# Image 0's mirrored runs moved to other steps, column sums in two chains of transfers, closings of layer 2 added from PSUM

## The chip, the cores and the metric

The kernel runs on one core of one Trainium2 chip. The metric is the device time of one execution in microseconds (us), the median of several runs. The engines are named as in the profile: PE (matmul), PEld (the loading of weights into PE), DVE (vector), ACT (activation), POOL (GpSimd) and SP (here a queue of DMA issues).

## The reference

Four images of 64 x 64 positions with 64 channels, float32, go through four layers one after the other:

```python
# layer 0: attention over the 4096 positions of an image, with q, k, v projections
energy = einsum('bic,bjc->bij', q, k); x = gamma * softmax(energy) @ v + x
# layer 1: a block of norm, pointwise, 3x3 depthwise taps, gate, channel scale, pointwise, and
#          a second half of norm, pointwise, gate, pointwise, each added to x
# layer 2: attention of the image with itself: softmax(x @ x.T) @ x, added to x
# layer 3: a non-local block (theta, phi, g projections), then a batch norm over all images
```

In layer 2 the scores are the product of x with itself, so the block of queries g against keys h is the transpose of the block of queries h against keys g. The kernel uses this: the exponential of one block serves both.

## The kernel before, in words

**Order of the work.** The kernel is a list of items that a schedule (lines 1790 to 1830) writes out by hand. Items 0 to 127 are layer 0, 32 per image. Layer 1 of an image is a generator that runs in a lane called `conv` inside the items that follow; each `yield` states how many us of item time are to pass before its next part. Layer 1 of image 3, the last one, runs inside image 0's layer 2. A second lane, `misc`, holds `features2` (keys of layer 2, tile `ko`), which are started at the item given in `misc_from`. Then come layer 2 of image 0, and layers 2 and 3 of the images by turns: 2(1), 3(0), 2(2), 3(1), 2(3), 3(2), 3(3).

**Layer 2.** The positions are cut into 8 parts. `PART` (image 0) and `FULL` (images 1 to 3) list, for each part h, which other parts are taken against it. A plain number g is one block that counts once; a pair in brackets is a mirrored run, whose blocks count for h and, transposed, for the two parts of the pair. Each number gives two steps, each pair four; image 0 has 100 steps and seven runs, the others 72 steps and fourteen runs each. `item(n)` (1484) issues for step n:

- `score(n)`: 4 matmuls (L1384; 8 records in the profile) into a PSUM slot of 128 x 1024, and two exponentials on ACT (L1389, with row sums) into half of an `e` tile. The slots are taken by turns (`new_ps`), and a matmul into a slot waits for the last reader of what was there.
- for a step of a run, `turned(n)`: a DVE transpose (L1402) into a `turned` tile; and `column_sums(n)`: in image 0 a DMA from POOL's queue that adds the exponentials into `esum` (L1417), in the others a POOL addition (L1419); after the last step of h one POOL addition joins the halves (L1421).
- `products(n)`, two steps later (three for the first of an h): 4 matmuls (L1440) into accumulators. At the end of an h the accumulators are copied or added to `A` (ACT copies at L1448 and, for image 0, L1451; DVE additions at L1454).
- `turned_products(run)`: 64 matmuls (L1465; 128 records) from the `turned` tile into two PSUM slots, and four DVE evacuations into `A` (L1478 additions, L1480 copies for the first visit). Within the pass the first two matmuls write the first slot and the next two the second one. Their other operand is `xr`, which `weights(h)` fetches in 16 transfers on SP (L1361) at the steps in `weights_at`.
- `spread_sums(h)`: a DVE transpose and a reduction of `esum` (L1429, L1430).

```python
for run, (_, _, last) in enumerate(runs):
    if n - (3 if b and run == 0 else 2) == last:
        turned_products(run)
```

**Pools.** `e`, `esum`, `own`, `xr` and layer 0's exponentials share a ring of six tiles, taken by turns. `turned`, `A`, `ko` and others share a ring of five big tiles. In image 0 the first six runs use one `turned` tile and the last another; in the other images two alternate. `t` tiles come from a ring of two.

**Layer 1 inside image 0's layer 2.** The depthwise taps are DVE instructions (L1240, with L1243 and L1251 as the last of a row), for r = 1 and then r = 0; `ytot` (L1257) sums their results, and a matmul at L1260 reads it. The second half is a norm (matmuls at L1170, transfers into `xn` at L1183) and pointwise matmuls (L1205), a DVE gate into `u` (L1288) and a matmul at L1292.

**Closing.** `close2(b)` (1517) finishes an image's layer 2 four blocks of 128 x 1024 at a time: 8 PE transposes of `A` into a PSUM slot (L1542), a DVE multiply by the reciprocal sums into a `t` tile (L1543), and two DVE additions to X (L1549). Images 0 to 2 are closed at items 12, 22, 32 and 42 of the next image's layer 2, two steps ahead of a turned pass; image 3 inside layer 3 of image 2.

Of the kernel before, what the change touches and what calls it, by code (L numbers as in the profile page):

```python
# [10 lines left out]
ALU = mybir.AluOpType  # L11
# [680 lines left out]
def fast_path(ctx: ExitStack, tc: tile.TileContext, a: dict, out: bass.AP, bad):  # L692
    nc = tc.nc
# [298 lines left out]
    def at(i, fn):  # L992
        due.setdefault(i, []).append(fn)
# [165 lines left out]
    def norm(x, y):  # L1159


        sq = [new_t("sq"), new_t("sq")]
        for i in range(2):
            act(sq[i], x[:, bass.ts(i, 1024)], AF.Square)
        yield 4.5
        ps = new_ps()
        for i, src in enumerate(((x, x), (sq[0], sq[1]))):
            for j in range(4):
                c = 512 * j if i == 0 else 512 * (j % 2)
                mm(  # L1170
                    ps[32 * j : 32 * j + 32, bass.ts(i, 512)], jsel, src[j // 2][:, c : c + 512],
                    start=True, stop=True,
                )
        t = new_t()
        act(t[:, 0:512], ps[:, 0:512], AF.Square)
        stt(t[:, 0:512], t[:, 0:512], -1.0, ps[:, 512:1024], ALU.mult, ALU.add)
        yield 4.0
        act(t[:, 0:512], t[:, 0:512], AF.Ln, bias=eps1)
        act(t[:, 512:1024], t[:, 0:512], AF.Exp, scale=-0.5)
        yield 3.0  # L1180
        for j in range(4):
            for h in range(2):
                nc.sync.dma_start(  # L1183
                    out=y[64 * h : 64 * h + 64, bass.ts(j, 512)],
                    in_=t[32 * j + 16 * h : 32 * j + 16 * h + 16, 512:1024]
                    .unsqueeze(1).to_broadcast([16, 4, 512]),
                )
        yield 11.0
        for jp in range(2):
            cols = bass.ts(jp, 1024)  # L1190
            nc.vector.tensor_mul(y[:, cols], y[:, cols], x[:, cols])
            yield 1.8
# [6 lines left out]
    def layer1(b):  # L1199
# [76 lines left out]
            nc.vector.tensor_add(xs, xs, t[:, 0:512])  # L1276
            yield 3.0
        z = xn.tile([128, 2048], F32, tag="xn", name="xn")
        yield from norm(x, z)
        for j in range(4):  # L1280
            t, u = new_t(), new_t("u")
            for r in range(2):
                ps = new_ps()
                pointwise(ps, pw3, r, z, j)
                if r == 0:
                    act(t, ps, AF.Identity, bias=pwb[:, 1, 0:1])
                else:
                    stt(u, ps, pwb[:, 1, 1:2], t, ALU.add, ALU.mult)  # L1288
                yield 6.0 if r else 4.0
            ps = new_ps()  # L1290
            for s in range(2):
                mm(ps[64 * s : 64 * s + 64, 0:512], pw4, u[:, bass.ts(s, 512)], start=True, stop=True)  # L1292
            act(t[:, 0:512], ps[:, 0:512], AF.Identity, bias=resb[:, 1:2], scale=V("L1_conv_gamma"))
            xs = x[:, bass.ts(j, 512)]
            nc.vector.tensor_add(xs, xs, t[:, 0:512])
            yield 3.0
# [3 lines left out]
    def features2(b):  # L1300
# [13 lines left out]
    SIDES = [[(7, (h + 1) % 7), ((h + 2) % 7, (h + 3) % 7)] for h in range(7)]  # L1314
    FULL = [(7, [7])] + [(h, [h] + SIDES[h]) for h in range(6)] + [(6, SIDES[6] + [6])]
    PART = [
        (0, [0, 5, (1, 2), 6, 7, (3, 4)]), (1, [1, 2, 3, 4, 7]), (2, [2, 1, 3, 4, 7]), (3, [3, 1, 2, 4]),
        (4, [4, 1, 2, 3]), (7, [7, 0, 5, 6, 1, 2, (3, 4)]), (6, [6, 0, (1, 2), 5, 7, (3, 4)]),
        (5, [5, 0, (1, 2), 6, (3, 4), 7]),
    ]  # L1320

    def layer2(b, when_free=None):
# [16 lines left out]
        m.first = [4 * sum(m.count[:g]) for g in range(8)]  # L1339
        m.mirrored = [h for h, _ in (PART if b == 0 else FULL) if mine_t[h]]  # L1340
        begin = [mine[h][0] for h in range(8)]
        spread_at = {mine_t[h][-1] + 5: h for h in m.mirrored}
        late_start = 4 if b else 6
        used, todo, seen = {}, [], set()
        st = {"e": {}, "T": {}, "esum": {}}

        def tile_of(run):
            return run % 2 if b else run // (len(runs) - 1)

        def slot(g, t):  # L1350
            k = used[g, t] = used.get((g, t), -1) + 1
# [12 lines left out]
                    )  # L1364

        if b == 0:
            weights_at = {0: 0, 24: 7, 44: 6, 74: 5}
        else:
            weights_at = {6: 0, 8: 1, **{mine[h][0] - 1: h for h in range(2, 7)}}

# [35 lines left out]
        def column_sums(n):  # L1406
            h, _, _, run, _ = steps[n]
            if run is None:
                return
            k, e = mine_t[h].index(n), st["e"][n]  # L1410
            if k == (0 if b == 0 else 1):
                st["esum"][h] = new_e("esum")
            if h not in st["esum"]:
                return
            esum = st["esum"][h][:, 0:1024]
            if b == 0:
                nc.gpsimd.dma_start(out=esum, in_=e, **({} if k == 0 else {"accum_op": ALU.add}))  # L1417
            else:
                nc.gpsimd.tensor_add(esum, st["e"][mine_t[h][0]] if k == 1 else esum, e)  # L1419
            if n == mine_t[h][-1]:  # L1420
                nc.gpsimd.tensor_add(esum[:, 0:512], esum[:, 0:512], esum[:, 512:1024])  # L1421
# [61 lines left out]
        def item(n):  # L1483
            if n in weights_at:
                weights(weights_at[n])
            score(n)
            turned(n)
            column_sums(n)
            todo.append(n)
            if n == 2:  # L1490
                m.A = new_big("A")
            if b == 0:
                follow(0)
                conv.tick(3.1)
                misc.tick(1.8)
            if n >= late_start:
                for _ in range(2):
                    if todo and todo[0] <= n - (3 if b == 0 and todo[0] in begin else 2):
                        products(todo.pop(0))
            for run, (_, _, last) in enumerate(runs):  # L1500
                if n - (3 if b and run == 0 else 2) == last:
                    turned_products(run)
                    if run == len(runs) - 2 and when_free:
                        when_free()
            if n == len(steps) - 1:
                while todo:
                    products(todo.pop(0))
            if n in spread_at:
                spread_sums(spread_at[n])
# [2 lines left out]
            items.append((lambda n=n: item(n), 1.6 if b else 0.0))  # L1512
        for n, h in spread_at.items():
            if n >= len(steps):
                at(len(items) + (1 if b else 6), lambda h=h: spread_sums(h))

    def close2(b):
        x, m = X[:, b], im[b]
        ps, tot, n = piece(), sums2[:, b, :], 4 * max(m.mirrored) + 4
        cs = m.cs.rearrange("p (j k) -> p j k", k=4)  # L1520
        for k in range(4):
            mm(ps[32 * k : 32 * k + 32, 0:n], sel4, cs[:, 0:n, k], start=True, stop=True)
        g = 0
        while g < 8:
            k = g
            while k < 8 and m.count[k] == m.count[g]:
                k += 1
            nc.vector.tensor_reduce(
                tot[:, 4 * g : 4 * k],
                m.zs[:, m.first[g] : m.first[g] + 4 * m.count[g] * (k - g)]  # L1530
                .rearrange("p (t k) -> p t k", k=m.count[g]), AX.X, ALU.add,
            )
            g = k
        nc.vector.tensor_add(tot[:, 0:n], ps[:, 0:n], tot[:, 0:n])  # L1534
        rz = sm.tile([128, 32], F32, tag="rz2", name="rz2")
        nc.vector.reciprocal(rz, tot)
        yield
        for i in range(4):
            ps, t = new_ps(), new_t()
            for j in range(8):  # L1540
                c = 1024 * i + 128 * j
                nc.tensor.transpose(ps[:, bass.ts(j, 128)], m.A[:, c : c + 128], ident)  # L1542
            nc.vector.tensor_mul(  # L1543
                t.rearrange("p (j n) -> p j n", n=128), ps.rearrange("p (j n) -> p j n", n=128),
                rz[:, bass.ts(i, 8)].unsqueeze(2).to_broadcast([128, 8, 128]),
            )
            xs = x[:, bass.ts(i, 512)].rearrange("p (j h) -> p j h", h=H)
            for o in range(2):
                nc.vector.tensor_add(xs, xs, t.rearrange("p (j o h) -> p j o h", j=8, o=2)[:, :, o, :])  # L1549
            yield  # L1550


# [251 lines left out]
    for b in range(B):  # L1804
        misc_to[len(items)] = True
        f = len(items)
        if b == 0:
            layer2(b)
            misc_from[f + 74] = [features2(b + 1)]
        else:  # L1810
            layer2(b, lambda b=b: keys3(b - 1))
            turns = close2(b - 1)
            for i in (8, 12, 22, 32, 42):
                at(f + i, lambda turns=turns: next(turns))
            misc_from[f + 46] = [open3(b - 1)]
            f = len(items)
            misc_to[f] = True
            layer3(b - 1)
            if b + 1 < B:
                turns = features2(b + 1)  # L1820
                for i in (4, 7, 10, 13):
                    between3[f + i] = 2, lambda turns=turns: next(turns)
# [221 lines left out]
```

## Time and profile before

| | |
|---|---|
| time, median of 3 runs | 2458.18 us (2457.44 to 2460.28) |
| profiled execution, its own time | 2460.18 us |
| span of the profiled execution | 2458.3 us |
| PE busy | 2414.6 us, 98% of the span |
| ACT, DVE, POOL busy | 67%, 60%, 21% |
| granted PE clock, mean | 0.996 |
| image 0's layer 2 | 1018 to 1277 us of the span |

The span runs from the first to the last instruction; the execution's own time has about 2 us around it. Busy time of PE is modelled, and matmuls overlap in it, so what a stall or an instruction costs is read from starts: a score or product of one step is 0.86 us of PE, a step that has nothing else 1.72 us. In a list of waits the columns are the waiting engine and line, what it waited for, the total, the number of times and the longest. In a timeline they are the start, the duration, the engine, line and operation, output and input, a count, and in brackets the idle time ahead of it with what ended it.

### The profile page before, as it was taken

Reading aid. Unit: us, or ns where it says so; the run is one execution under the profiler, and the core shown is the slowest. Engines: PE = TensorE matmul, PEld = TensorE weight load, DVE = VectorE, ACT = ScalarE, POOL = GpSimd, SP = SyncE. Lnnn points to the kernel's source line nnn. Section 1 sums busy time; section 2 is a strip of 40 time slices with the busy share of each in tenths; the row PEclk is TensorE's granted clock in tenths of the full one; section 3 lists DMA queues with packets and bytes.
Section 4 is the critical chain, followed back from the end, with each engine's and each line's share of the span. In section 5 each row is a group of like instructions: output and inputs, shape, how many; then the busy total and the mean of one; then the engine's idle time right before and its main releaser. Section 6 shows DMA issues by size and latency. Waiting matters only on the chain.

```text
span 2458.3 us, 63648 instructions
## 1 busy us (share of the span) xinstructions
PE 2414.6 (98%) x27509; PEld 932.0 (38%) x27509; DVE 1471.1 (60%) x1785; ACT 1648.8 (67%) x3144; POOL 528.0 (21%) x379
## 2 busy tenths in 40 slices
PE   9999999999999999999899999999999999999998
PEld 3343453336433633335334442144431244421113
DVE  2010377227822773278547757877668876678886
ACT  4666766676666666678454449964479844579996
POOL 2000000000000000000127662247631365622110
PEclk9999999999999999999999999999999999999999
DMA  3000000000000000230540017610065400296554
GB/s 79 1 18 1 19 1 18 18 19 1 18 18 18 2 19 18 50 65 18 112 102 22 19 45 155 135 31 19 20 138 118 91 19 20 68 174 139 121 117 117
DMA packets 67094, 134.31 MB, mean 55 GB/s; under 512 B 12941, under 2 KB 34166, under 8 KB 66806
## 3 DMA queue, kind: packets, MB, share of 16 engines
q0 software_dynamic: 23744, 84.46, 17.2%
q1 hardware_dynamic: 42309, 43.85, 7.9%
q8 instruction: 218, 3.57, 0.6%
q10 hardware_dynamic: 752, 1.85, 0.2%
q14 instruction: 71, 0.57, 0.1%
HBM read 4.80 MB, written 4.19 MB: 4 GB/s over the span
## 4 chain that ended last, share of the span: by engine, by line
PE 85%; DVE 7%; ACT 4%; DMA 2%; issue 1%; SPq 0%; POOL 0%; ACTq 0%; DVEq 0%; POOLq 0%
PE PS L1121 18%; PE PS L1095 18%; PE PS L1384 9%; PE PS L1440 9%; PE PS L1627 8%; PE PS L1688 8%; PE PS L1465 7%; PE PS L1205 2%; DVE tg L1679 2%; DVE y L1240 2%; ACT e L1638 2%; DMA xn<-e 1%; ACT e L1389 1%; DVE turned L1402 1%; ACT e L1100 1%
## 5 line engine op out<-in xcount | busy, mean ns | idle before, releaser
L1100 ACT ACTIVATE e<-PS 128x1024 f32<-128x1024 f32 x512 | 523.6, 1023 | 332.3 <-PE PS L1095 299.6
L1389 ACT ACTIVATE e<-PS 128x512 f32<-128x512 f32 x632 | 370.8, 595 | 350.8 <-PE PS L1384 330.6
L1121 PE MATMUL PS<-e,vq 64*64 64x512 f32 x4096 | 577.2, 592 | 0.0
L1095 PE MATMUL PS<-X,q 64*64 64x512 f32 x4096 | 574.9, 590 | 1.8 <-DVE X L979 1.7
L1638 ACT ACTIVATE e<-PS 128x512 f32<-128x512 f32 (+2 forms) x588 | 500.1, 921 | 58.3 <-PE PS L1627 35.8
L1679 DVE TENSOR_TENSOR tg<-tg,e 128x2048 f32<-128x2048 f32 x172 | 393.9, 2290 | 42.8 <-ACT e L1638 31.4
L1384 PE MATMUL PS<-ko 64*64 64x512 f32 x2528 | 343.4, 596 | 2.9 <-DVE A L1480 2.0
L1440 PE MATMUL PS<-e,X 64*64 64x512 f32 x2528 | 339.7, 594 | 1.4 <-DVE X L1133 0.6
L1240 DVE SCALAR_TENSOR_TENSOR y<-pad,vec,y 128x1024 f32<-128x1024 f32 x240 | 307.9, 1283 | 14.8 <-ACT y L1236 7.4
L1419 POOL TENSOR_TENSOR esum<-esum,e 128x1024 f32<-128x1024 f32 x126 | 298.9, 2372 | 49.3 <-ACT e L1389 42.3
L1402 DVE STREAM_TRANSPOSE turned<-e 128x1024 f32<-128x1024 f32 x196 | 241.0, 1238 | 114.0 <-ACT e L1389 114.0
L1627 PE MATMUL PS<-tg,ph 32*64 32x512 f32 x4096 | 294.9, 612 | 1.4 <-ACT e L1638 1.2
L1417 POOL DMA_DIRECT2D esum<-e x28 | 23.1, 827 | 1222.3 <-ACT e L1389 1171.4
L1095 PEld LDWEIGHTS PS<-X,q 64*64 64x64 f32 x4096 | 184.0, 133 | 258.9 <-issue 178.5
L1121 PEld LDWEIGHTS PS<-e,vq 64*64 64x64 f32 x4096 | 184.1, 133 | 252.0 <-issue 158.7
L1688 PE MATMUL PS<-e,tg 128*32 128x512 f32 x2048 | 272.5, 604 | 0.0
L1108 DVE TENSOR_REDUCE sums<-zs 128x1 f32<-128x4 f32 x128 | 19.6, 153 | 260.6 <-ACT e L1100 260.4
L1440 PEld LDWEIGHTS PS<-e,X 64*64 64x64 f32 x2528 | 105.6, 134 | 171.2 <-issue 148.3
L1660 POOL DMA_DIRECT2D xn<-e x116 | 101.1, 897 | 289.9 <-ACT e L1638 205.0
L1384 PEld LDWEIGHTS PS<-ko 64*64 64x64 f32 x2528 | 98.0, 133 | 164.3 <-issue 135.2
L1465 PE MATMUL PS<-turned,xn 32*64 32x256 f32 x5376 | 156.3, 377 | 0.5 <-DVE sums L1534 0.5
L1627 PEld LDWEIGHTS PS<-tg,ph 32*64 32x64 f32 x4096 | 63.4, 129 | 222.5 <-ACT e L1638 191.5
(217 smaller groups left out, 1685.0 us busy)
## 6 DMA issues: line engine op xcount, KB each, us to landing
xn<-e POOLq DMA_DIRECT2D x132, 512.0 KB, 5.2
esum<-e POOLq DMA_DIRECT2D x28, 512.0 KB, 4.6
xn<-X SPq DMA_DIRECT2D x336, 32.0 KB
xn<-t SPq DMA_DIRECT2D x64, 128.0 KB
ph<-tg SPq DMA_DIRECT2D x64, 128.0 KB
ko<-ko SPq DMA_DIRECT2D x32, 128.0 KB
xr<-in_x_dram SPq DMA_DIRECT2D x13, 256.0 KB
q<-q SPq DMA_DIRECT2D x12, 256.0 KB
```

Of the source, the lines that this page charges most:

```text
L1095: mm(ps[64 * c : 64 * c + 64, bass.ts(r, 512)], m.q[rows_, 128 * t + 64 * c : 128 * t + 64 * c + 64], x[rows_, bass.ts(g, 512)], start=Tru ...
L1100: act(es[g // 2][:, bass.ts(g % 2, 1024)], ps, AF.Exp, bias=SHIFT0, accum_out=zs[:, g : g + 1],)
L1121: ins = mm(PS[64 * s : 64 * s + 64, 2048 + 512 * j : 2560 + 512 * j], vq[rows_, :], es[j // 2][rows_, k : k + 512], start=t == 0 and i < 2 ...
L1240: stt(y1, win, wt, y1, ALU.mult, ALU.add)
L1384: mm(ps[64 * c : 64 * c + 64, bass.ts(r, 512)], m.ko[rows_, k : k + 64], m.ko[rows_, bass.ts(h, 512)], start=True, stop=True,)
L1389: act(e[:, bass.ts(r, 512)], ps[:, bass.ts(r, 512)], AF.Exp, bias=SHIFT2, accum_out=slot(g, 2 * u + r),)
L1440: mm(st["acc"][r][64 * c : 64 * c + 64, :], xw[rows_, 4 * g + 2 * u + c, :], st["e"][n][rows_, bass.ts(c, 512)], start=n == mine[h][0], st ...
L1465: mm(slots[q // 2][64 * c : 64 * c + 64, o : o + 256], st["xr"][rows_, w : w + 64], T[rows_, bass.ts(e, 256)], start=e < 2, stop=e >= 14,)
L1627: mm(PS[64 * c : 64 * c + 64, bass.ts(banks[k], 512)], m.ph[32 * k : 32 * k + 32, 128 * mc + 64 * c : 128 * mc + 64 * c + 64], m.th[32 * k ...
L1638: act(e[:, 512 * lo : 512 * k], PS[:, 512 * banks[lo] : 512 * banks[lo] + 512 * (k - lo)], AF.Exp,)
L1679: nc.vector.tensor_add(esum, esum, e)
L1688: mm(st["y"][32 * k : 32 * k + 32, :], m.gx[:, i % 32, :], es[i][:, bass.ts(k, 512)], start=mc == 0, stop=i % 32 == 31,)
```

## The change

Seven things change, all but the last in image 0's layer 2:

1. `PART` orders the blocks anew. The runs before end at steps 7, 15 (h 0), 67 (h 7), 75, 83 (h 6), 91 and 97 (h 5); afterwards at 5, 13 (h 0), 23 (h 1), 77, 83 (h 6), 91 and 97 (h 5). The number of blocks, steps and runs in the table is the same.
2. Two `turned` tiles alternate, and each turned pass is issued three steps after its run's last step instead of two. The last step of the layer is 99.
3. The weights are fetched at steps 0, 10, 40 and 50.
4. The column sums of an h go by turns to two halves of `esum`, two chains of transfers, and one more transfer joins them: 32 issues instead of 28. `spread_sums` comes nine steps after the last step of a run instead of five.
5. `features2(1)` starts at step 82 instead of 74.
6. The second half of layer 1 of image 3 states 1.3 times its us at each `yield` (`far`).
7. `close2` of all images writes the multiply back to its PSUM slot, takes no `t` tile, and both additions read PSUM.

```diff
         z = xn.tile([128, 2048], F32, tag="xn", name="xn")
-        yield from norm(x, z)
+        far = 1.3 if b == B - 1 else 1.0
+        for us in norm(x, z):
+            yield far * us
...
-                yield 6.0 if r else 4.0
+                yield (6.0 if r else 4.0) * far
...
     PART = [
-        (0, [0, 5, (1, 2), 6, 7, (3, 4)]), (1, [1, 2, 3, 4, 7]), (2, [2, 1, 3, 4, 7]), (3, [3, 1, 2, 4]),
-        (4, [4, 1, 2, 3]), (7, [7, 0, 5, 6, 1, 2, (3, 4)]), (6, [6, 0, (1, 2), 5, 7, (3, 4)]),
-        (5, [5, 0, (1, 2), 6, (3, 4), 7]),
+        (0, [0, (1, 2), 7, 5, (3, 4), 6]), (1, [1, 2, (5, 6), 3, 4, 7]), (2, [2, 1, 3, 4, 7]),
+        (3, [3, 1, 2, 4, 7]), (4, [4, 1, 2, 3, 7]), (7, [7, 0, 1, 2, 3, 4]),
+        (6, [6, (2, 3), 0, (4, 7), 5]), (5, [5, (2, 3), 0, (4, 7), 6]),
     ]
...
-        spread_at = {mine_t[h][-1] + 5: h for h in m.mirrored}
+        spread_at = {mine_t[h][-1] + (5 if b else 9): h for h in m.mirrored}
...
         def tile_of(run):
-            return run % 2 if b else run // (len(runs) - 1)
+            return run % 2
...
-            weights_at = {0: 0, 24: 7, 44: 6, 74: 5}
+            weights_at = {0: 0, 10: 1, 40: 6, 50: 5}
...
             if b == 0:
-                nc.gpsimd.dma_start(out=esum, in_=e, **({} if k == 0 else {"accum_op": ALU.add}))
+                both = st["esum"][h]
+                nc.gpsimd.dma_start(
+                    out=both[:, bass.ts(k % 2, 1024)], in_=e, **({} if k < 2 else {"accum_op": ALU.add})
+                )
+                if n == mine_t[h][-1]:
+                    nc.gpsimd.dma_start(out=esum, in_=both[:, 1024:2048], accum_op=ALU.add)
...
             for run, (_, _, last) in enumerate(runs):
-                if n - (3 if b and run == 0 else 2) == last:
+                if n - (3 if b == 0 or run == 0 else 2) == last:
                     turned_products(run)
...
-                at(len(items) + (1 if b else 6), lambda h=h: spread_sums(h))
+                at(len(items) + (1 if b else 8), lambda h=h: spread_sums(h))
...
-            ps, t = new_ps(), new_t()
+            ps = new_ps()
...
+            blocks_ = ps.rearrange("p (j n) -> p j n", n=128)
             nc.vector.tensor_mul(
-                t.rearrange("p (j n) -> p j n", n=128), ps.rearrange("p (j n) -> p j n", n=128),
-                rz[:, bass.ts(i, 8)].unsqueeze(2).to_broadcast([128, 8, 128]),
+                blocks_, blocks_, rz[:, bass.ts(i, 8)].unsqueeze(2).to_broadcast([128, 8, 128])
             )
...
-                nc.vector.tensor_add(xs, xs, t.rearrange("p (j o h) -> p j o h", j=8, o=2)[:, :, o, :])
+                nc.vector.tensor_add(xs, ps.rearrange("p (j o h) -> p j o h", j=8, o=2)[:, :, o, :], xs)
...
-            misc_from[f + 74] = [features2(b + 1)]
+            misc_from[f + 82] = [features2(b + 1)]
```

In the kernel after, the same lines are found a little lower: L1384 is L1386 there, L1389 is L1391, L1440 is L1447, L1465 is L1472, L1542 is L1549, L1543 is L1551 and L1549 is L1556.

## The prediction

> **What bounds it now.** The page comes first: PE is busy nearly all the span and carries the chain.
>
> ```profile
> PE 2414.6 (98%) x27509; PEld 932.0 (38%) x27509; DVE 1471.1 (60%) x1785; ACT 1648.8 (67%) x3144; POOL 528.0 (21%) x379
> PE 85%; DVE 7%; ACT 4%; DMA 2%; issue 1%; SPq 0%; POOL 0%; ACTq 0%; DVEq 0%; POOLq 0%
> ```
>
> So only PE instructions removed and PE stalls made or removed change the time. Second, the waits of PE in image 0's layer 2 (1018 to 1290 us; total, times, longest):
>
> ```profile
> PE PS L1465 <- DVE turned L1402: 6.5, 1, 6.5
> PE PS L1205 <- ACT e L1389: 2.1, 1, 2.1
> PE PS L1384 <- DVE A L1480: 2.0, 1, 2.0
> PE PS L1292 <- DVE u L1288: 1.7, 1, 1.7
> PE PS L1170 <- ACT sq L1164: 1.2, 1, 1.2
> ```
>
> Third, stretches of the span behind the third and the first of these (busy time and instructions of PE, weight loads, DVE, ACT and POOL, then the granted PE clock, DMA share and GB/s):
>
> ```profile
> 1072.50:1077.00 4.50, 4.50 (x28) 1.45 (x30) 4.36 (x6) 1.26 (x4) 0.77 (x1) 0.62 0.78 149
> 1172.10:1179.00 6.90, 5.63 (x112) 3.65 (x120) 4.46 (x9) 0.00 (x0) 1.90 (x2) 0.51 0.43 81
> ```
>
> Behind a long stall PE runs at about half clock, so the stall costs twice. A step of this layer is a score (L1384) and a product (L1440) of 0.86 us each, so the starts of the scores show what a stall costs with its slow stretch. Step 70 starts 14.78 us after step 69, where 1.72 and a turned pass of 3.6 to 4.1 would do: 8.9 lost at L1402. The same count gives 3.9 at L1480 (steps 18 to 20), and for the tail from step 76 on 1.75 at L1170, 3.96 at L1205 (with half clock), 1.88 at L1292 and 0.85 behind step 99: 8.4.
>
> Fourth, the timeline of one closing in image 1's layer 2, and two groups of additions:
>
> ```profile
> 1305.68 0.49 PE L1542 MATMUL PS<-ident,A 128*128 128x128 f32 x3
> ...
> 1306.21 1.23 DVE L1543 TENSOR_TENSOR t<-PS,rz 128x1024 f32<-128x1024 f32 x1 [1.04 <-PE PS L1542]
> ...
> 1307.47 1.55 DVE L1549 TENSOR_TENSOR X<-X,t 128x512 f32<-128x512 f32 x2
> ...
> 1307.98 2.39 PE L1465 MATMUL PS<-turned,xn 32*64 32x256 f32 x77
> ```
> ```profile
> L1549 DVE TENSOR_TENSOR X<-X,t x32: 691/693/1621, 1307.5 to 2174.2; 128x512 f32<-128x512 f32 x32
> L1454 DVE TENSOR_TENSOR A<-PS,A x46: 652/691/693, 1071.0 to 2137.3; 128x512 f32<-128x512 f32 x46
> ```
>
> The multiply ends at 1307.43, and the turned pass that reuses its slot starts at 1307.98: 0.55 us of slack.
>
> [...] The trace shows half clock for 3.41 or 6.83 us, but already behind stalls of 2.0 and 2.1 us; gaps of 1.2 to 1.7 us caused none. [...] L1549, both operands in SBUF, takes 0.82 or 1.62 us in 12 of 32 instances, where POOL adds; L1454, one operand in PSUM, 0.68 with POOL busy or not. The two medians show no PSUM surcharge.
>
> **The closings (+12.8 us).** The slot was released by the multiply; now by the second addition, since both read PSUM. Per block: two additions at 0.69 with gaps of 0.04 and 0.03 are 1.45 us behind the multiply. The third matmul of the next turned pass writes that slot, so it waits 1.45 less 0.56, plus about 0.05 for the release (what L1627 took behind L1543): 0.95 us. Everything on PE is queued behind it, scores and products of the following steps first, and ACT's exponentials wait for those. All 12 blocks of images 0 to 2 have the same slack, 0.56: 12 x 0.95 = 11.4. Image 3's four blocks run in layer 3 with other banks: their additions end 0.2 us ahead of the next writer three times; the fourth multiply starts late behind L1679, its addition ends 1.39 after the writer's start: 1.4 more. Bounds: no trace shows DVE writing PSUM. [...] Additions at 0.65 save 1; image 3's may vanish; contention as in L1549 would add up to 9. From 10.5 to 22; I take 12.8, because L1454 shows no contention. DVE's saving on L1549 is off the path.
>
> **A pass that is no longer issued (-3.6, with a new wait -3.0).** In image 0 the turned pass now runs at n - 3 == last. The last run, h 5 with parts 4 and 7, ends at step 97, so its pass would fall at n = 100, past the last step, 99. The instruction lists agree: 13,904 matmuls before, 13,840 after, 64 fewer, which is one pass, and 4 evacuations fewer. That run's mirrored products are left out. Its price stands in the timeline of PE before:
>
> ```profile
> 1271.83 3.71 PE L1465 MATMUL PS<-turned,xr 32*64 32x256 f32 x128
> 1275.47 1.95 PE L1440 MATMUL PS<-e,X 64*64 64x512 f32 x16
> ```
>
> From start to start 3.64 us, all on the path. It also covered ACT's lag; without it, scores 102 to 104 (0.86 each on PE, 1.27 on ACT) wait some 0.6. Bounds 2 to 3.6.
>
> **Steps 2 to 7 (+5).** The column-sum tile comes from the ring of six e tiles at step 2, formerly 4. So step 4's tile is the one that layer 0's last product reads, and that L1121 starts at 1030.77, behind score 5. Step 4's exponentials, at 1029.33 before, wait for it, and ACT has to do them, L1178, L1179 and step 5's in order (1.58, 0.72, 0.63, 1.58 us):
>
> ```profile
> 1030.77 1.09 PE L1121 MATMUL PS<-e,vq 64*64 64x512 f32 x8
> ...
> 1031.77 0.58 ACT L1389 ACTIVATE e<-PS 128x512 f32<-128x512 f32 x1
> ...
> 1032.49 1.23 PE L1384 MATMUL PS<-ko 64*64 64x512 f32 x5 [0.63 <-ACT e L1389]
> ```
>
> Score 6 moves from 1032.5 to about 1036, products(0) as far: +3.2 to 3.5, and an idle time of 4 us can halve the clock: 1.7, or 3.4. Bounds 3.2 to 6.9; I take 5.
>
> **The other runs of image 0.** No number of steps or products changes; places do.
> - Steps 16 to 20: the copies L1480 no longer stand behind taps (L1240, 1.32 us each); two taps remain ahead of one addition, 1.4 instead of 3.9: -2.5.
> - The new run in h 1, steps 20 to 23, lies inside the taps that it was to leave. Each of its four transposes (1.24) stands behind two taps: 1.7 us late; its evacuation, behind four taps, holds score 28 another 1.35: +3.05. Bounds 1.5 to 6.5 (half clock).
> - Steps 64 to 70: the stall of 6.5 goes with the run of h 7. Next comes L1260 at step 70, on ytot, the end of all taps: 2.0 after the start of step 43, plus 53.7 us of DVE before, less four transposes, 50.8, up to 51.3 with the moved additions; PE arrives 47.35 after it. Wait 3.5 to 4.1, half clock 1.7 to 3.4: 5.2 to 7.5 for 8.9, so -2.2 (-1.5 to -3.7).
> - The accumulator copies of h 6 and 5 (L1451) cost ACT's lag: +0.5 (0 to 1).
> - The tail: `far` spaces image 3's layer 1, so xn is there ahead of L1205 and u ahead of L1292; the late features2 put its copies behind two transposes of DVE, 1 to 2.5. About 3.4 for 8.4: -5. Bounds 0 (the same waits elsewhere) to -7.
> - The two chains and the joining transfer: 32 issues on POOL for 28, 0.57 to 0.9 us each; POOL is 21% busy, and spread_sums comes four steps later, more than the 4.5 to 5 us that a joining transfer takes to land. On SP the first 32 transfers of L1361 stand ahead of layer 1's in both; the last 16 come at step 50, not 74, ahead of nothing in the tail. Zero; if POOL's join came late, `cs` is only needed at step 108: still zero.
>
> **Sum.** 12.8 - 3.0 + 5 - 2.5 + 3.05 - 2.2 + 0.5 - 5 = +8.65. Against the profiled execution's own 2460.18 (span 2458.3) that is 2468.8; it lies 2.0 above the median 2458.18, so the median becomes about 2466.8.
>
> **Rivals.**
> - Not slower: the closings don't stall. The place is the third matmul of the 12 passes; it decides if the additions end within 0.6 us of the multiply, 0.3 each. Against: no 128x512 addition is under 0.65. For: nothing. Then 2466.8 - 12.8 = 2454.0.
> - The moved runs bring more: no wait at step 6 (if the ring's buffer is free sooner), tail -7, step 70 -3.7: 8.65 - 5 - 2 - 1.5 = 0, 2458. For: the copies of the tail may be hidden.
> - Half clock behind more gaps (step 6 whole, h 1, L1260): + 1.7 + 3.4 + 1.7: 2473.6. For: two gaps of 2.0 and 2.1 us did it.
> - PSUM operands contend after all, or the write is slow: + up to 9, 2476.
> - That the pass is issued elsewhere would add 3.6; the lists say it isn't.
>
> **How the numbers follow.** A measurement here tells about 0.2%, 4.9 us, from no change. Likeliest case 0.55 (2462 to 2471), half clock 0.18, moved runs better 0.16, contention 0.06, no stall at the closings 0.05. Slower by over 4.9, above 2463.1: nine tenths of the first (0.50) and both dear cases (0.24), 0.74. Faster, under 2453.3: some of the last case and of what the moved runs could give beyond their rival's sum, 0.04. The rest is 0.22. The range runs from just under the rival in which the moved runs bring more to just above half clock and the nearer part of contention; the case without stalls, half of contention and the far ends of the others stay out: 2457 to 2476.
>
> **What would show it.** Right: a PE wait of about 0.9 us on DVE's addition to X, 12 times, at L1472; turned passes of image 0 six times; score 6 near 1036; L1260 waiting 3 to 4 us on ytot; no wait on `turned` over 2. Wrong: no such repeated wait, or an execution under 2455; then the slot was free. [...]

## The result, and the profile after

The changed kernel takes 2468.52 us (median of 6 runs, 2466.94 to 2469.53), the kernel before beside it 2459.2 (2457.22 to 2461.23). The ratio is 1.0038, interval 1.0025 to 1.0051: slower by some 9.3 us, where 2466.8 was forecast. The profiled execution has a span of 2467.7 us against 2458.3. The changed kernel leaves out the mirrored products of one run, about 3.6 us of PE; that is work not done and not a gain.

The page's first lines and its chain of work, after:

```profile
PE 2419.8 (98%) x27381; PEld 919.5 (37%) x27381; DVE 1464.7 (59%) x1784; ACT 1649.7 (67%) x3144; POOL 531.5 (22%) x383
PE 84%; DVE 9%; ACT 4%; issue 1%; SPq 1%; DMA 0%; DVEq 0%; ACTq 0%
```

PE has 128 records fewer (one turned pass) and yet is busy 5 us longer, and DVE's share of the chain went from 7 to 9%: PE waits for DVE in more places. Part of its work runs at half clock behind its longer waits (0.50 and 0.51 in the windows below); the mean granted clock is 0.996, as before. The longest waits of PE from 1018 to 1300 us (total, times, longest):

```profile
PE PS L1260 <- DVE ytot L1257: 3.9, 1, 3.9
PE PS L1386 <- ACT e L1391: 3.2, 1, 3.2
PE PS L1529 <- DVE cs L1437: 3.2, 1, 3.2
PE PS L1386 <- DVE A L1487: 1.6, 1, 1.6
PE PS L1472 <- DVE turned L1404: 1.1, 1, 1.1
```

The wait of 6.5 us on `turned` is gone. In its place stand three of 3.2 to 3.9 us, each with a slow stretch behind it. These windows pair each wait, in order of time, with what follows (columns as in the prediction: busy time of PE, PEld, DVE, ACT, POOL, then the granted clock):

```profile
1031.60:1037.20 5.60, 2.40 (x21) 0.78 (x14) 3.06 (x4) 3.66 (x10) 1.27 (x2) 1.00 0.46 102
1037.20:1040.70 3.50, 3.50 (x20) 0.80 (x16) 1.92 (x3) 1.27 (x4) 0.50 (x1) 0.51 1.05 198
1176.60:1180.60 4.00, 0.61 (x8) 0.00 (x0) 3.89 (x6) 1.47 (x6) 0.00 (x0) 1.00 0.00 0
1180.50:1187.40 6.90, 6.29 (x30) 2.26 (x34) 0.90 (x5) 1.27 (x4) 0.00 (x0) 0.51 0.00 0
1285.60:1289.70 4.10, 0.91 (x20) 0.25 (x14) 3.68 (x9) 1.08 (x4) 4.02 (x2) 1.00 0.21 53
1289.80:1293.20 3.40, 3.40 (x20) 1.04 (x20) 0.88 (x3) 1.27 (x4) 0.33 (x2) 0.50 0.19 49
```

Now one closing in image 1's layer 2, as a timeline, with the groups of its two DVE lines:

```profile
1303.29 1.23 DVE L1551 TENSOR_TENSOR PS<-PS,rz 128x1024 f32<-128x1024 f32 x1 [1.04 <-PE PS L1549]
...
1304.56 1.42 DVE L1556 TENSOR_TENSOR X<-PS,X 128x512 f32<-128x512 f32 x2
...
1305.06 0.65 PE L1472 MATMUL PS<-turned,xn 32*64 32x256 f32 x4
...
1306.03 2.60 PEld L1472 LDWEIGHTS PS<-turned,xn 32*64 32x64 f32 x102 [0.78 <-DVE X L1556]
1306.03 2.84 PE L1472 MATMUL PS<-turned,xn 32*64 32x256 f32 x94 [0.32 <-DVE X L1556]
```
```profile
L1556 DVE TENSOR_TENSOR X<-PS,X x32: 691/691/693, 1304.6 to 2182.7; 128x512 f32<-128x512 f32 x32
L1551 DVE TENSOR_TENSOR PS<-PS,rz x16: 1224/1231/1233, 1303.3 to 2180.7; 128x1024 f32<-128x1024 f32 x16
```

The pass starts at 1305.06, issues two matmuls (4 records), and stops until 1306.03, just after the second addition ends at 1305.98. From start to start that is 0.97 us, although PE's own idle time is listed as 0.32: the four records are modelled as busy for 0.65 of it. The list of PE's waits over the whole span has it 12 times:

```profile
PE PS L1472 <- DVE X L1556: 3.8, 12, 0.3
```

The additions take 0.69 us in all 32 instances, also in the 21 that overlap an addition on POOL. Before, with both operands in SBUF, 12 of them overlapped one, and these took 0.82 to 1.62.

A clearer measure is the time from one image's first closing transposes to the next image's. They start at 1305.08, 1637.89, 1970.77 and 2153.56 before, and at 1302.16, 1638.80, 1975.43 and 2162.05 after. Over the first three intervals the difference grows by 3.83, 3.75 and 3.83 us, so the four blocks of one image cost 3.8 us; to the end of the span, in which image 3 is closed, it grows by 0.94 more. All of it together is 12.35. Up to the first of them the changed kernel is 2.92 us ahead.

### The profile page after: what moved, and what is told of

The parts are those of the page before. It is cut to its first block, busy times and chain, and to the rows that moved or that the text cites. A ratio compares the mean times of both kernels' runs of the same rounds, so it can differ in the third digit from the quotient of the medians.

```text
span 2467.7 us, 63393 instructions
## 1 busy us (share of the span) xinstructions
PE 2419.8 (98%) x27381; PEld 919.5 (37%) x27381; DVE 1464.7 (59%) x1784; ACT 1649.7 (67%) x3144; POOL 531.5 (22%) x383
## 4 chain that ended last, share of the span: by engine, by line
PE 84%; DVE 9%; ACT 4%; issue 1%; SPq 1%; DMA 0%; DVEq 0%; ACTq 0%
PE PS L1121 18%; PE PS L1095 17%; PE PS L1386 9%; PE PS L1447 9%; PE PS L1634 8%; PE PS L1695 8%; PE PS L1472 7%; DVE tg L1686 3%; PE PS L1205 2%; DVE y L1240 2%; ACT e L1645 2%; ACT e L1100 1%; DVE X L1556 1%; ACT e L1391 1%; PE PS L1170 1%
## 5 line engine op out<-in xcount | busy, mean ns | idle before, releaser
L1391 ACT ACTIVATE e<-PS 128x512 f32<-128x512 f32 x632 | 371.0, 595 | 366.1 <-PE PS L1386 338.5
L1121 PE MATMUL PS<-e,vq 64*64 64x512 f32 x4096 | 577.5, 592 | 0.0
L1386 PE MATMUL PS<-ko 64*64 64x512 f32 x2528 | 345.4, 600 | 4.9 <-ACT e L1391 3.2
L1447 PE MATMUL PS<-e,X 64*64 64x512 f32 x2528 | 341.6, 597 | 1.3 <-ACT own L1458 0.8
L1634 PE MATMUL PS<-tg,ph 32*64 32x512 f32 x4096 | 294.8, 612 | 1.7 <-ACT e L1645 0.8
L1121 PEld LDWEIGHTS PS<-e,vq 64*64 64x64 f32 x4096 | 184.4, 133 | 251.7 <-issue 157.9
L1472 PE MATMUL PS<-turned,xn 32*64 32x256 f32 x5376 | 163.9, 377 | 4.3 <-DVE X L1556 3.8
L1447 PEld LDWEIGHTS PS<-e,X 64*64 64x64 f32 x2528 | 100.9, 134 | 178.9 <-issue 156.6
L1386 PEld LDWEIGHTS PS<-ko 64*64 64x64 f32 x2528 | 93.6, 133 | 174.2 <-issue 147.1
L1634 PEld LDWEIGHTS PS<-tg,ph 32*64 32x64 f32 x4096 | 63.4, 129 | 222.6 <-ACT e L1645 190.2
```

The lines of the kernel that those rows point to most:

```text
L1121: ins = mm(PS[64 * s : 64 * s + 64, 2048 + 512 * j : 2560 + 512 * j], vq[rows_, :], es[j // 2][rows_, k : k + 512], start=t == 0 and i < 2 ...
L1386: mm(ps[64 * c : 64 * c + 64, bass.ts(r, 512)], m.ko[rows_, k : k + 64], m.ko[rows_, bass.ts(h, 512)], start=True, stop=True,)
L1391: act(e[:, bass.ts(r, 512)], ps[:, bass.ts(r, 512)], AF.Exp, bias=SHIFT2, accum_out=slot(g, 2 * u + r),)
L1447: mm(st["acc"][r][64 * c : 64 * c + 64, :], xw[rows_, 4 * g + 2 * u + c, :], st["e"][n][rows_, bass.ts(c, 512)], start=n == mine[h][0], st ...
L1472: mm(slots[q // 2][64 * c : 64 * c + 64, o : o + 256], st["xr"][rows_, w : w + 64], T[rows_, bass.ts(e, 256)], start=e < 2, stop=e >= 14,)
L1634: mm(PS[64 * c : 64 * c + 64, bass.ts(banks[k], 512)], m.ph[32 * k : 32 * k + 32, 128 * mc + 64 * c : 128 * mc + 64 * c + 64], m.th[32 * k ...
```

## The experiments

All ratios are to the kernel before, timed beside each variant on the same chip. Differences to the changed kernel are between medians taken on different chips and at different times, and loose by one to two microseconds: the medians of the kernel before range from 2458.2 to 2460.1.

**The closings, undone and alone.**

```diff
-            ps = new_ps()
+            ps, t = new_ps(), new_t()
...
-                blocks_, blocks_, rz[:, bass.ts(i, 8)].unsqueeze(2).to_broadcast([128, 8, 128])
+                t.rearrange("p (j n) -> p j n", n=128), ps.rearrange("p (j n) -> p j n", n=128),
+                rz[:, bass.ts(i, 8)].unsqueeze(2).to_broadcast([128, 8, 128]),
...
-                nc.vector.tensor_add(xs, ps.rearrange("p (j o h) -> p j o h", j=8, o=2)[:, :, o, :], xs)
+                nc.vector.tensor_add(xs, xs, t.rearrange("p (j o h) -> p j o h", j=8, o=2)[:, :, o, :])
```

> The changed kernel with the closings of before (multiply into a t tile, additions from it), all else as changed. Theory (the slot held for two more additions costs 12 x 0.95 us in layers 2 and about 1 us in layer 3): 12.3 us under the changed kernel, that is some 2456, a ratio to before near 0.9985, and no passes of L1472 interrupted after their second matmul. Rival (the profile lists only 3.8 us of PE idle time on these additions, and the rest of the loss lies in the moved runs): some 2464, a ratio near 1.002.

Measured: 2455.26 us, ratio 0.9983 (0.9976 to 0.9989). And the reverse, the same edit of the diff made on the kernel before:

> The kernel before with only the closings changed (multiply back into the PSUM slot, both additions from it). Theory: 11.4 us of stalls in the 12 passes behind closings and 0.9 to 1.4 in layer 3: 12.3 us over before, some 2471.5, ratio 1.005. Rival (idle time as the profile lists it): +4.5, ratio 1.0018.

Measured: 2471.91 us, ratio 1.0049 (1.0032 to 1.0066). The first lies 13.3 us under the changed kernel; the second 0.49%, 12.0 us, over the one before (13.6 between their medians). Both agree with 12.3 within that looseness, and not with 4. In the second, who waited for the additions:

```profile
  PEld PS L1465: 9.3, 12
  PE PS L1465: 3.9, 12
  PEld PS L1627: 1.6, 1
  PE PS L1627: 0.7, 1
```

Twelve passes, as the prediction said, and one place in layer 3. The first of the two also shows that everything else together is a gain of some 4 us (0.17%), about as much as the pass that is left out.

**The pass that is not issued.** In every variant of the changed kernel that doesn't say otherwise, the mirrored products of image 0's last run are left out, as there. This one issues them.

```diff
-                if n - (3 if b == 0 or run == 0 else 2) == last:
+                if n - (3 if (b == 0 and run < len(runs) - 1) or run == 0 else 2) == last:
```

> The changed kernel with the turned pass of image 0's last run issued two steps after its last step, at step 99, so that no pass is missing. Theory (a pass is 3.64 us of PE, and in return it covers waits of the next scores of some 0.6): +3.0 to +3.6 over the changed kernel, some 2471.8, ratio to before 1.0052. Rival (the pass fills PE time that is idle anyway in front of the sums of the closing at L1529, 3.2 us of wait and the slow stretch behind it): +0 to +1, some 2469, ratio 1.004.

Measured: 2472.95 us, ratio 1.0051 (1.0034 to 1.0067); the span grew from 2467.7 to 2472.0. The pass costs its full 3.64 us: the starts of the scores on either side of it are 8.1 us apart, against 4.3 in the changed kernel. The wait at L1529 is 3.2 us in both and was not filled by it. The rest of the 4.3 us are differences between the two executions: the mean granted clock was 0.995 here and 0.996 in the changed kernel's, and layer 2 of image 0 started 0.8 us earlier.

**The last column sums.**

```diff
-                at(len(items) + (1 if b else 8), lambda h=h: spread_sums(h))
+                at(len(items) + (1 if b else 5), lambda h=h: spread_sums(h))
```

> The changed kernel with the last spread_sums of image 0 three items earlier (5 items into image 1's layer 2, not 8). Theory (the sums are late because L1436 stands on DVE behind the transposes of steps 106 to 108, which wait for ACT; the transfers had joined long before): the wait of 3.2 us at L1529 and the half clock behind it go, -4 to -5 us from the changed kernel, some 2464, ratio 1.002. Rival (the joining transfer and POOL's addition are what is late): the wait stays, 2468.5.

Measured: 2463.36 us, ratio 1.0017 (1.0010 to 1.0023), 5.2 us under the changed kernel; the wait at L1529 is gone, and the mean granted clock of the profiled execution is 0.997 against 0.996. The timeline of the changed kernel shows why it was there:

```profile
1272.40 1.27 POOL L1428 TENSOR_TENSOR esum<-esum 128x512 f32<-128x512 f32 x1 [3.77 <-DMA esum<-esum]
...
1285.10 1.23 DVE L1404 STREAM_TRANSPOSE turned<-e 128x1024 f32<-128x1024 f32 x1
...
1286.71 1.25 DVE L1404 STREAM_TRANSPOSE turned<-e 128x1024 f32<-128x1024 f32 x1 [0.39 <-ACT e L1391]
1287.88 0.67 DVE L1436 STREAM_TRANSPOSE esum<-esum 128x512 f32<-128x512 f32 x1
1288.59 0.69 DVE L1437 TENSOR_REDUCE cs<-esum 128x16 f32<-128x512 f32 x1
...
1289.42 0.29 PE L1529 MATMUL PS<-cs,sel 128*32 128x28 f32 x8 [3.19 <-DVE cs L1437]
```

The sums were joined at 1273.7. Their spreading stood on DVE behind the transposes of image 1's first steps, in the order of issue, and reached DVE 14 us later, right ahead of the matmul that needs it.

**The first run.** Its steps moved back by one part, the tile of column sums is taken at step 4 again:

```diff
-        (0, [0, (1, 2), 7, 5, (3, 4), 6])
+        (0, [0, 7, (1, 2), 5, (3, 4), 6])
```

> The changed kernel with the first run of h 0 back at steps 4 to 7 (part 7 taken ahead of the pair 1, 2), so that the column-sum tile is taken from the ring of e tiles at step 4 again. Theory (the step at which that tile is taken makes step 4's exponentials wait for layer 0's last product): the wait of 3.2 us at step 6 and the 3.4 us at half clock go, -3.6 us from the changed kernel, some 2464.9. Rival (the wait comes from the transposes of the earlier run on DVE ahead of layer 0's last additions): -1 at most, as the transposes of steps 4 and 5 stand there again.

Measured: 2468.55 us, ratio 1.0035 (1.0022 to 1.0048): no gain. The wait at step 6 did go (score 6 starts 0.6 us late, as before), but this one came:

```profile
PE PS L1205 <- issue: 3.7, 1, 3.7
```
```profile
1047.62 1.22 DVE L1191 TENSOR_TENSOR xn<-xn,X 128x1024 f32<-128x1024 f32 x1 [7.52 <-DMA xn<-t]
...
1048.94 2.10 PE L1205 MATMUL PS<-xn,pw 64*64 64x512 f32 x8 [3.70 <-issue]
```

Layer 1's first pointwise matmul needs `xn`, whose transfers stand on SP behind 32 weight transfers (issued from 1013.83 to 1035.84, those of `xn` from 1036.01). In the kernel before, the pass of the first run was issued ahead of L1205, at step 9, and its 3.64 us of PE covered the time. With the run at steps 4 to 7 and three steps of lag the pass comes behind L1205. The wait is not the same in every execution: the complete variant further down has the same instructions up to here, and in its profile `xn` came sooner and PE idled 1.1 us; the next products started 0.88 us after L1205 there, and 1.73 us after it here. The run's step and its pass's lag thus hang together, which the next variant tests by giving that pass its old lag:

```diff
-                if n - (3 if b == 0 or run == 0 else 2) == last:
+                if n - (3 if (b == 0) == (run > 0) else 2) == last:
```

> The changed kernel with the first run back at steps 4 to 7 and its turned pass two steps after its last step, at step 9, as in the kernel before; the other passes as changed. Theory (with the run moved back alone, the wait at step 6 went, but the pass came behind L1205 instead of ahead of it, and PE stood 3.7 us for layer 1's transfers into xn that the pass had covered): both waits are gone, -3.5 to -4.5 us from the changed kernel, some 2464.5. Rival (the wait on xn is set by SP's 32 weight transfers ahead of it and stays wherever the pass is): 2468.

Measured: 2464.59 us, ratio 1.0023 (1.0014 to 1.0032), 3.9 under the changed kernel; of both waits 0.6 us is left. The edit moves the run's transposes together with its column-sum tile, so the time alone does not part them. The timeline of the changed kernel does: step 4's exponential waited for layer 0's last product (L1121), the reader of the e tile that comes round to it, and not for DVE.

```profile
1032.84 0.60 ACT L1391 ACTIVATE e<-PS 128x512 f32<-128x512 f32 x1 [3.13 <-PE PS L1121]
```

**Closings one step earlier.**

```diff
-            for i in (8, 12, 22, 32, 42):
+            for i in (8, 11, 21, 31, 41):
```

> The changed kernel with the four blocks of each closing of images 0 to 2 issued one step earlier (items 11, 21, 31, 41), additions still from PSUM. The closing's slot then comes round as the first of the pass, but one step (1.72 us) later. Theory (0.95 us per pass is a lack of slack between the additions and the pass, which one step more than covers): -11 us from the changed kernel, some 2457.2, ratio to before 0.9993. Rival (reading or writing PSUM from DVE slows PE's own writes, or the delay moves to the scores that take the slots sooner): little or no gain, 2465 or more.

Measured: 2457.1 us, ratio 0.9990 (0.9983 to 0.9996), 11.4 under the changed kernel, which is 12 x 0.95. The additions still read PSUM and take 0.69 each, and no matmul of a turned pass (PE, L1472) is left among those that waited for them:

```profile
  PEld PS L1472: 9.7, 12
  PEld PS L1634: 1.6, 1
  PE PS L1634: 0.7, 1
```

The first two intervals between closings are 332.81 and 332.80 us, as in the kernel before (332.81 and 332.88). So in layers 2 it is slack alone, and no cost of PSUM itself shows. Image 3's closing, in layer 3, was not moved and keeps its wait (L1634).

**The matmul on ytot later.**

```diff
-        yield 7.0
+        yield 13.0 if b == B - 1 else 7.0
```

> The changed kernel with the yield behind ytot at 13 us instead of 7 for image 3, so that the matmul on ytot (L1260) comes two steps later, at step 72. Theory (PE stands at L1260 for the end of the taps, 3.9 us, and half clock behind it costs 3.4 more): -5 to -7.3 us, some 2462, if what follows in layer 1 has two steps of room. Rival (layer 1's second half is then late itself, and the waits at L1170, L1205 or L1309 grow by as much): 0 to -2.

Measured: 2463.1 us, ratio 1.0017 (1.0011 to 1.0024), 5.4 under the changed kernel. The wait at L1260 fell from 3.9 to 0.5, the mean granted clock of the profiled execution rose from 0.996 to 0.997, and the second half of layer 1 had the room.

**One chain of transfers.**

```diff
-                nc.gpsimd.dma_start(
-                    out=both[:, bass.ts(k % 2, 1024)], in_=e, **({} if k < 2 else {"accum_op": ALU.add})
-                )
+                nc.gpsimd.dma_start(out=esum, in_=e, **({} if k == 0 else {"accum_op": ALU.add}))
```

> The changed kernel with image 0's column sums in one chain of transfers per h, as before, and no joining transfer; times of the sums as changed. Theory (the transfers have slack of many steps in either form, and L1436 is late through DVE's queue): no change, 2468.5 within 1 us, the wait at L1529 still 3.2 us. Rival (the two chains are what lets the sums be ready): 5 to 10 us slower; or the joining transfer is what costs: 3 us faster.

Measured: 2478.75 us, ratio 1.0080 (1.0065 to 1.0094): 10 us slower, against the theory. What ACT waited for, in this variant from 1018 to 1320 us:

```profile
ACT e L1391 <- PE PS L1386: 79.6, 55, 6.9
ACT e L1391 <- DMA esum<-e: 9.8, 2, 7.0
```

The second line does not occur in the changed kernel. A transfer of a chain waits for the one before it to land (they are mostly issued 5.0 to 5.7 us apart; into `esum` a transfer took a median of 4.8 us to land in the changed kernel), while the steps of a run come every 1.7 to 3 us, so the chain falls behind. Each `e` tile stays taken until its transfer has read it, so ACT can't write the next. PE's longest new wait, 6.4 us at the products (L1442), falls into the 7.0 us in which ACT stands, and the mean granted clock is 0.994 against 0.996. The kernel before has one chain too, its transfers also 5 us apart, and ACT waits for none of them there. So the two chains earn their place in the new order; which runs stand too close together was not tried.

**All repairs at once.** The last pass issued, the sums three items earlier, the first run later, the closings one step earlier, L1260 later:

> All of these on the changed kernel at once: last pass issued at step 99, last spread_sums three items earlier, first run at steps 4 to 7, closings one step earlier, L1260 two steps later. Theory (the costs are separate places on PE and add): 2468.5 + 3.6 - 4.7 - 3.6 - 11 - 6 = some 2446.8, ratio to before 0.995. Rival (a wait removed early comes back later in image 0's layer 2, since layer 1's chain on DVE and ACT sets that stage's length): 2452 or more.

Measured: 2450.63 us, ratio 0.9968 (0.9958 to 0.9979), with executions from 2449.2 to 2457.4. It missed its 2446.8 by 3.8 us. The forecast took 3.6 us off for the first run, which moved alone had gained nothing; the other four repairs, as measured alone, would give some 2451. That the earlier pass would bring the rest is not shown: the last variant below has it and is 1.0 us faster. Two variants set the lags of the passes. In the first, the lags of first, third and last pass are 2, 4 and 2:

> The kernel with all changes of the complete one before it (last pass issued, last sums three items earlier, first run at steps 4 to 7, closings one step earlier, L1260 two steps later), and the passes of the first, third and last run at lags of 2, 4 and 2 steps. Theory: the wait of 1.1 us at L1205 (step 10) is covered by the pass again, and the transposes of the run in h 1 have ended when its pass starts (1.1 us); -2 us from the complete one's 2450.6, some 2448.5, ratio to before 0.9960. Rival (the third pass's evacuation then stands behind more taps and holds a later score by as much): no change, 2450.6.

Measured: 2453.72 us, ratio 0.9982 (0.9974 to 0.9990): by the medians 3.1 us slower than the one it was to improve, with intervals that just touch. Its waits show the rival's mechanism, larger than supposed:

```profile
PE PS L1386 <- DVE A L1487: 4.7, 1, 4.7
```

The transposes had ended when the third pass began, but its evacuation now stood behind more of the taps: 4.7 us instead of 1.7, and behind it three scores and products started 1.6 to 1.8 us apart instead of 0.86. With that pass back at three steps:

> The complete kernel (last pass issued, last sums three items earlier, first run at steps 4 to 7, closings one step earlier, L1260 two steps later) with the first pass at a lag of two steps and the last at two, all others of image 0 at three. Theory (in the variant with the third pass at four, its evacuation stood behind more taps, 4.7 us and the half clock behind it; without that the first pass's cover of 1.1 us at L1205 is left): -1 to -2 us from 2450.6, some 2449.3, ratio to before 0.9963, which is not to be told from the complete kernel. Rival (the earlier first pass is what made the variant slower): some 2453.

Measured: 2449.61 us, ratio 0.9958 (0.9945 to 0.9972), all passes issued. It beats both kernels and the variant with the third pass at four steps, so that lag was the loss; from the complete variant it can't be told apart.

## Why the prediction was right, and where it was not

The sum was +8.65, the spans differ by 9.4 and the medians by 9.3. In the table a loss is what the starts on PE exceed the undisturbed durations of the same groups in a stretch, before and after, so that slow clock is in it.

| step of the prediction | predicted | measured |
|---|---|---|
| closings in layers 2 | +11.4 | +11.4 |
| closings in layer 3 | +1.4 | +0.9 |
| the pass not issued | -3.6, with a new wait -3.0 | -3.6, no new wait in the list |
| steps 2 to 7 | +5 | +3.6 (loss 2.2, then 5.9) |
| steps 16 to 20 | -2.5 | -2.9 (4.1, then 1.1) |
| the run in h 1 | +3.05 | +2.6 (0.6, then 3.2) |
| steps 64 to 71 | -2.2 | -2.5 (10.0, then 7.5) |
| accumulator copies | +0.5 | +1.2 |
| the tail, to step 99 | -5 | -6.9 (10.9, then 4.0) |
| column sums at image 1's start | 0 | +4.3 (1.7, then 6.0) |

The rows add up to +8.1. The changed kernel's profiled execution started image 0's layer 2 0.8 us later (1018.95 against 1018.15), after the same instructions; that is no part of the change: with one more pass and nothing else altered, another execution started it at 1018.19.

**The closings** were right in place, number and size: the slack of 0.55 us, 1.45 us of additions, twelve passes. The choice among the bounds was right too: additions that read PSUM took 0.69 beside POOL's as well, and the multiply that writes PSUM took 1231 ns against 1224, 7 more. Undoing them and doing them alone both moved the time by about this amount; one step earlier took away the part in layers 2. That a rearrangement of image 0 wins in all, but only some 4 us with a pass left out, is what the other rows say.

**The two chains and `spread_sums`** are where a step failed. They were put at zero with the words that "`cs` is only needed at step 108". That looked at POOL and at the transfers, which did have slack, and not at DVE, where the moved `spread_sums` is issued behind the transposes of step 108, directly ahead of its reader. It cost 4.3 us by the starts; moving it three items earlier brought 5.2. Going through DVE's queue as the prediction did for POOL's and SP's would have found it. The same bullet took the two chains as a mere four issues more; one chain in the new order is 10 us slower, so they are needed there.

**The tail and steps 2 to 7** came out 1.9 and 1.4 us better than their terms. At step 6 the score moved by 3.5 us (1032.49 to 1036.00), as forecast, but 0.8 of that is the layer's later start. The stall itself grew by 2.7: from layer 0's last product to score 6 it was 1.72 us and became 4.43. So the working was too high by 0.5 to 0.8, and 1036.00 was hit in part by luck. The slow window of 3.41 us (from 1037.2 on, at 0.51) cost the low value of 1.7, and the wait of 0.6 of products(0) in the kernel before was taken up in the new one. In the tail the waits of 1.7 and 2.1 us at L1292 and L1205 left nothing behind. These terms and the failed step cancel, so the closeness of the total is in part luck.

**The mechanism at step 6** was right, its remedy incomplete: undone alone it gave nothing, because the wait at L1205 took its place. In both kernels the time in which `xn` arrives is covered by the first pass, which is issued ahead of L1205 (at 1044.59 before, at 1046.56 in the changed kernel); moving the run back at a lag of three steps takes that cover away.

**What was to show it.** Six passes of image 0, score 6 at 1036.00 (with the help of the later start), a wait of 3.9 us on ytot and no wait over 2 us on `turned`: all there. The "PE wait of about 0.9 us" came 12 times but is listed as 0.3.

## What to carry to other kernels

A tile that is read where it lies saves a buffer and holds its own place longer; look for the slack ahead of its next writer before making the edit, and move the work one step earlier if it is less than the added readers take. When a step is moved, ask on every engine what is queued ahead of it at its new place, the engine that was not thought of included. A wait that is removed can uncover the next one: undo edits in pairs when one gives nothing. Compare waits by what they add between two starts, not by the time at which something happens, since an execution can be early or late as a whole.

## What the runs showed of the hardware that was not expected

- The idle time listed for PE can be a third of what a stall costs: 0.32 us listed where the starts are 0.97 apart, because the matmuls ahead of it are modelled as busy. The weight loads listed as waiting are no measure either: with closings one step earlier they still waited 9.7 us in 12 passes on the additions, and no time was lost.
- Half clock came in stretches of 3.41 and 6.83 us. Before: 3.41 us at 0.50 from 1073.1 behind the wait of 2.0, 6.83 from 1172.1 behind that of 6.5, 3.41 from 1223.3 behind that of 2.1. In the changed kernel: 3.41 from 1037.2 and from 1289.8 behind the two waits of 3.2, 6.83 from 1180.6 behind that of 3.9. In the rest of the span from 1018 to 1290 us before, and to 1310 us after, the clock was 1.00, behind waits of 1.2 and 1.7 us before and of 1.1 and 1.6 after as well. Executions of one kernel differ: over the 25 of the kernel before beside the one-chain variant the mean granted clock ran from 0.994 to 0.997 and the time from 2454.05 to 2463.2. What decides it was not shown.
- In the best variant's profiled execution no wait of PE from 1018 to 1310 us is over 1.7 us, and the mean granted clock over the span is 0.999, against 0.996 in the kernels before and after.
- One chain of accumulating transfers, issued 5 us apart, showed no wait of ACT in the old order and cost 10 us in the new one, where ACT waited 9.8 us for it in two places: the wait is for the tiles that its sources hold, not for its result (PE's wait on `cs` stayed at 3.2 us).
